# Residual and last MLP bias by accumulating DMA, and GpSimd in written order, in a one-core kernel of delta attention, MLP and gated feed-forward

## The chip, the cores and the metric

The kernel runs on one core of one Trainium2 chip. A core has five engines with a queue of instructions each: TensorE (PE, matmul; its weight loads are listed as PEld), VectorE (DVE), ScalarE (ACT), GpSimd (POOL) and SyncE (SP), which here only issues DMA transfers. An engine works its queue in order; between engines there are semaphores. The metric is the device time of one execution in microseconds; of a kernel, the median of its runs.

## What is computed

For each of 32 sequences of 512 tokens with 256 features, in float32:

```
x1 = layernorm(x)
x2 = x1 + delta(layernorm(x1)*dn_g + dn_b)            # q, k, v, rates lr; k normalized
     K = tril(k k^T, -1);  u = solve(I + K, v);  y = (q k^T)(lr * u);  y @ out_w + out_b
x3 = x2 + relu((layernorm(x2)*mn_g + mn_b) @ w1 + b1) @ w2 + b2
y  = x + x3                                           # the residual of the first half
out = y + (silu(h @ wg^T) * (h @ wu^T)) @ wd^T        # h = layernorm(y); wg, wu, wd: integers / 127
```

The change concerns the terms `x` and `b2` of `y`, which is held in the tile `a` of each sequence and becomes the output.

## The kernel before

Sequences go in pairs; there are 16. A tile is 128 partitions (tokens of a block) by 4 blocks by 256 features. Three pairs are in the machine at a time: the *older* pair ends its gated part (its down projection, `Down`), the *old* pair goes through MLP and gated part, the *new* pair through attention, and a *following* pair is loaded and normalized. `a` has six buffers, one for each sequence of three pairs.

The stages of one round, in the order in which the program writes them:

- `middle` (L1055): the down projections of the older pair (`plain` L976, `combined` L993) among the MLP of the old pair (`residual` L900, `mlp_in` L905, `mlp_out` L923, then `normed` and `turned` for stage "f"). Inverting the 32x32 blocks of the new pair (`invert` L632, on VectorE: L683, L689) is spread between as a side job (`Side`, paid by TensorE columns).
- `gated` (L931): gate and up products of the old pair, the longest stretch of matmuls (L940), then interleaved with `solution` (L1032), the block substitution of the new pair (`merge` L712, `solve` L770). In it a matmul `pr` is followed by `rhs` on VectorE (L788) and then by the matmul `pu` that reads it. As a side job the following pair is normalized (`normalized` L483).
- `values_phase` (L1174): the rest of the attention of the new pair, its layer norm for the MLP (`normed`, stage "m"), keys and Gram matrices of the following pair, whose diagonal blocks go through DRAM (`given`) to the inversion.

A layer norm that feeds a matmul ends in a transposition: VectorE turns 32x32 blocks (`Turn.chunk`, L460), SP writes them to DRAM (`way_m`, `way_f`, `way_a`) and fetches them as features by tokens (`hT_m`, `hT_f`, `ag`). Its reciprocal square root is on GpSimd (`r_m`, `r_f`, `rr`, L391), with a small product after it (`mr_m`, `mr_f`, L419).

In `normalized` the last feature of each token is replaced in `a` by a number that later products need; the feature itself is kept in `hlast` (L522, L523: two copies for each of four blocks) and put back in `gather` (L817).

`x` is loaded a second time for the residual (`fetch_residual`, L893, at the start of `values_phase`); GpSimd adds `b2`, spread over the partitions in `b2s`, and VectorE adds the tile to `a` in `residual`.

The down projection uses products of sums of blocks: `plain` multiplies the blocks of `hid` as they are, after which GpSimd replaces them by sums and differences (L987 to L990) for `combined`; GpSimd also adds parts of the result to `a` (L991, L1005, L1006).

What sets the order: TensorE, VectorE, ScalarE and SP execute in the order in which the program writes their instructions (`manual_schedule`, L1231). GpSimd is not in that list: a scheduler places its instructions, and had, for instance, moved L987 forward into the gated stage.

```
with tc.manual_schedule(engines={
    mybir.EngineType.PE, mybir.EngineType.DVE, mybir.EngineType.Activation, mybir.EngineType.SP
}):
```

Of the kernel before, what the change touches and what calls it, by code (L numbers as in the profile page):

```python
# [15 lines left out]
P = 128  # L16
# [6 lines left out]
def kernel(  # L23
# [297 lines left out]
    wdS = const.tile([P, NP, 7, P], F32, name="wdS")  # L321

    class Dequant:
        def __init__(self, src, name, tag, bufs, k):

            rows, self.cols = src.shape
            self.name, self.parts = name, []
            for r0 in range(0, rows // P, k):
                m = min(k, rows // P - r0)
                wi = wk.tile([P, m, self.cols], I32, tag=tag, name=f"{name}_i{r0}", bufs=bufs)  # L330
                self.parts.append((r0, m, wi))
            self.src = src

# [149 lines left out]
    def normalized(s):  # L483

        n = s.n
        mv = yield from stats(s.a, f"a{n}")


        vv = small.tile([P, 2, NT], F32, tag="vv", name=f"vv_{n}")
        nc.vector.tensor_scalar(vv[:, 0, :], mv[:, :, 1], EPS, None, ALU.add)  # L490
        nc.vector.scalar_tensor_tensor(
            out=vv[:, 1, :], in0=vv[:, 0, :], scalar=EPS, in1=mv[:, :, 1],
            op0=ALU.mult, op1=ALU.add,
        )
# [3 lines left out]
        nc.vector.tensor_scalar(nm, mv[:, :, 0], -1.0, None, ALU.mult)  # L498
# [12 lines left out]
        nc.vector.tensor_tensor(both, rr[:, 0, :], rr[:, 1, :], ALU.mult)  # L511
        s.r2 = small.tile([P, 2, NT], F32, tag="r2", name=f"r2_{n}", bufs=5)
        nc.vector.tensor_tensor(
            s.r2, vv, both.unsqueeze(1).to_broadcast([P, 2, NT]), ALU.mult
        )
        s.hlast = small.tile([P, NT, 1], F32, tag="hlast", name=f"hlast_{n}", bufs=5)
        for c in range(NT):
            nc.vector.tensor_scalar(
                s.a[:, c, :], s.a[:, c, :], left[:, c : c + 1], rr[:, 0, c : c + 1],
                ALU.subtract, ALU.mult,  # L520
            )
            nc.gpsimd.tensor_copy(s.hlast[:, c, :], s.a[:, c, C - 1 : C])  # L522
            nc.gpsimd.tensor_copy(s.a[:, c, C - 1 : C], s.r2[:, 1, c : c + 1])  # L523
            yield
        if n // NS == 1:
            s.ag = wk.tile([P, NF, T], F32, tag="aT", name=f"ag_{n}")
        else:
            s.ag = wk.tile([P, NF, T], F32, tag="feat", name=f"ag_{n}", bufs=4)
        if n >= 2 * NS:
            t = Turn(f"a{n}")  # L530
            for c in range(NT):
                t.chunk(s.a[:, c, :], c)
                yield
            t.send()
            for _ in range(4):
                yield
            t.fetch(s.ag)
        yield
# [74 lines left out]
    def norms(g, given, seqs):  # L613

        ss = small.tile([P, NS, NT], F32, tag="ss", name=f"ss_{g}", bufs=2)
        nc.sync.dma_start(
            ss.rearrange("p s t -> p (s t)"),
            given.rearrange("s b i e -> (s b) (i e)")[:, :: B + 1].rearrange("q t -> t q"),
        )
        yield  # L620
        yield 4
        kn = small.tile([P, NS, NT], F32, tag="kn", name=f"kn_{g}", bufs=2)
        nc.gpsimd.tensor_tensor(
            kn.rearrange("p s t -> p (s t)"), ss.rearrange("p s t -> p (s t)"), half, ALU.pow
        )
        yield 4
        for slot, s in enumerate(seqs):
            s.kn = kn[:, slot, :]
            nc.vector.tensor_tensor(s.kn, s.kn, s.r2[:, 0, :], ALU.mult)
        yield  # L630
# [259 lines left out]
        else:  # L890
            s.turn.fetch(s.hT)

    def fetch_residual(s):  # L893
        s.xt = wk.tile([P, NT, C], F32, tag="x", name=f"x_{s.n}")
        load_x(s.n, s.xt)
        nc.gpsimd.tensor_tensor(
            s.xt, s.xt, b2s.unsqueeze(1).to_broadcast([P, NT, C]), ALU.add
        )

    def residual(s):  # L900

        s.acc = s.a
        nc.vector.tensor_tensor(s.acc, s.acc, s.xt, ALU.add)

    def mlp_in(s, o):  # L905
        n = s.n
# [45 lines left out]
    class Down:  # L952
# [23 lines left out]
        def plain(self):  # L976
# [5 lines left out]
            x = wk.tile([P, 2, P], F32, tag="x2", name=f"x2_{name}")  # L982
            nc.scalar.copy(x, po[:, 1:3, :])
            first = self.acc[:, :, :P]

            A = self.A
            nc.gpsimd.tensor_tensor(A[1, 0], A[1, 0], A[1, 1], ALU.add)  # L987
            nc.gpsimd.tensor_tensor(A[0, 0], A[1, 0], A[0, 0], ALU.subtract)
            nc.gpsimd.tensor_tensor(A[0, 1], A[0, 1], A[0, 0], ALU.subtract)
            nc.gpsimd.tensor_tensor(A[1, 1], A[1, 1], A[0, 0], ALU.subtract)  # L990
            nc.gpsimd.tensor_tensor(first, first, x, ALU.add)  # L991

        def combined(self):  # L993
            name = f"{self.s.n}_{self.half}"
# [57 lines left out]
            next(gen)  # L1052
        return gens

    def middle(old, rest):  # L1055
# [21 lines left out]
        turned(one, "f")  # L1077
        todo(second[2:3])
        normed(two, "f")
        todo(second[3:])  # L1080
        return [d.store for d in rest]

    def last_middle(old, rest):
        one, two = old
        residual(one)
        rest[0].combined()
        mlp_in(one, 0)
        mlp_in(one, 1)
        residual(two)
        rest[1].combined()  # L1090
        mlp_out(one, 0)
        mlp_out(one, 1)
# [12 lines left out]
    def first_values(seqs, following, norms_, inverse, given):  # L1105
# [37 lines left out]
        for _ in turns:  # L1143
            pass
        for s in seqs:
            fetch_residual(s)
        whole = lambda gen: [None for _ in gen]
        whole(gather(one))
        whole(gather(two))
# [23 lines left out]

    def values_phase(seqs, following, prep, given, downs_left):  # L1174
        one, two = seqs
        for s in seqs:
            fetch_residual(s)
        whole = lambda gen: [None for _ in gen]
        if not following:
            units = iter(downs_left)  # L1180
            whole(gather(one))
            whole(gather(two))
            whole(through_values(one))
            next(units).plain()
# [5 lines left out]
            next(units).plain()  # L1190
            turned(one, "m")
            answer(two)
            normed(two, "m")
            next(units).plain()
            next(units).plain()
            turned(two, "m")
            return
        a, b = following
# [18 lines left out]
        keys(b, 0)  # L1217
        keys(b, 1)
        normed(one, "m")
        answer(two)  # L1220
        in_order(b)
        some(3)
# [6 lines left out]
        return sides_  # L1229

    with tc.manual_schedule(engines={  # L1231
        mybir.EngineType.PE, mybir.EngineType.DVE, mybir.EngineType.Activation, mybir.EngineType.SP
    }):

        first = pairs[0]
        gw = [wk.tile([P, GC], F32, tag="a", name=f"gw{f}", bufs=6) for f in range(NF)]
        quantized = [
            (Dequant(w_down, "wd", "hid", 2, 2), Combined().put),
            (Dequant(w_gate, "wg", "turn", 2, 4), whole_rows(wgT)),
            (Dequant(w_up, "wu", "x", 2, 4), whole_rows(wuT)),  # L1240
        ]
        load_a(first[0])
        gates = Gates(gw)
# [9 lines left out]
        b2s = const.tile([P, C], F32, name="b2s")  # L1253
        nc.scalar.dma_start(b2s, b2.partition_broadcast(P))
        for _ in normalized(first[0]):
            pass
        to_keys(first[0])
# [19 lines left out]
        for g in range(n_pairs):  # L1277
# [6 lines left out]
            else:  # L1284
                rest = downs(older) if older else []
                turned(old[1], "m")
                kn_side = Side(begun_[0], 10, 16 * 1024)
                inv_side = Side(
                    begun_[1], B * (4 + 3 * B // 2),
                    INVERT if older else INVERT_FIRST,  # L1290
                )
                stores = middle(old, rest)
                work = gated(old)
                for i in range(PLAIN):
                    next(work)
# [24 lines left out]
        for i, _ in enumerate(work):  # L1320
            if i == 5:
                turned(old[1], "f")
            if i in (3 * NH, 3 * NH + 2):
                rest.append(Down(old[0], len(rest)))
                rest[-1].plain()
        for h in range(NT // 2):
            rest.append(Down(old[1], h))
            rest[-1].plain()
        for d in rest:
            d.combined()  # L1330
            d.store()
# [29 lines left out]
```

## Time and profile before

| | us |
|---|---|
| median of 3 runs (2092.58, 2093.53, 4598.82) | 2093.53 |
| the profiled execution | 2090.19 |
| its span, first to last instruction | 2088.4 |
| mean granted TensorE clock | 0.995 of full |

Groups that the change touches (line, engine, count, busy us, mean ns):

| what | engine | count | busy us | mean ns |
|---|---|---|---|---|
| L896 x + b2 | POOL | 32 | 74.6 | 2348 |
| L903 a + x | DVE | 32 | about 48 (32 at the median of 1502) | 1502 |
| L522, L523 last feature | POOL | 128 + 128 | 34.3 + 26.5 | 268, 207 |
| L817 last feature back | POOL | 32 | 6.2 | 193 |
| L987 to L990 sums of blocks | POOL | 4 x 64 | 63.1, 79.5, 64.0, 64.0 | 1007 to 1243 |
| L991, L1005, L1006 result | POOL | 3 x 64 | 47.4, 33.0, 64.0 | 741, 516, 1000 |
| L623 kn | POOL | 16 | 31.3 | 1958 |

Transfers (KB each, median us from issue to landing): `x` 512, 5.5; `a` 512, 4.6; `hT_m` 512, 3.6; `hT_f` 512, 3.8; `ag` 512, 3.8; `blocks` 512, 5.1; `way_m` 128, 3.4; `given` 16, 1.5. GpSimd itself issues two transfers, both in the first 12 us: `row` (4 KB, 749 ns on the engine, 2.3 us to landing) and `unit` (128 KB, 659 ns, 5.4 us).

How to read it: a row of a group or a timeline gives start, duration, engine and line, operation, what is written from what, and in brackets how long the engine was idle before it and who released it. A wait row gives the total in us, the number of times and the longest. In a row of stretches the busy us of PE, PEld, DVE, ACT and POOL are followed by the granted clock, the share of the 16 DMA engines and GB/s. The ends of matmuls are modelled, and GpSimd's durations are rough.

### The profile page before, as it was taken

The numbers are of one execution on the slowest core, as the hardware profiler recorded it, in microseconds if no ns is written. First come the engines' busy times: TensorE is split into PE (matmuls) and PEld (weight loads), VectorE is DVE, ScalarE is ACT, GpSimd is POOL, SyncE is SP. The second block draws the span as 40 slices with busy tenths as digits, with TensorE's granted clock in tenths as the row PEclk, the third lists the DMA queues.
The fourth block names the chain that finished last, engine by engine and source line by source line (L and its number), as shares of the span: only waits on it lengthen the run. The fifth ranks groups of instructions, "written<-read, shape, count | busy, mean of one in ns | idle before, by whom it ended". The sixth has DMA issues, their size and how long they took to land.

```text
span 2088.4 us, 27547 instructions
## 1 busy us (share of the span) xinstructions
PE 2028.3 (97%) x9134; PEld 1373.5 (66%) x9134; DVE 1232.8 (59%) x3691; ACT 703.9 (34%) x1788; POOL 729.9 (35%) x1008
## 2 busy tenths in 40 slices
PE   5899999999999999999999999999999999999998
PEld 2565766757576675766767576675766767576675
DVE  3656474755747576474855747476474855747252
ACT  3333423324242343423334242343423334242231
POOL 3411332525224342432525224251422525124244
PEclk9999999999999999999999999999999999999999
DMA  3211332332324223332332324223332432323020
GB/s 90 83 34 28 84 98 62 109 90 56 91 71 127 63 74 89 92 90 62 107 95 54 94 69 128 62 74 89 87 95 62 113 88 54 94 69 107 22 61 21
DMA packets 249605, 163.90 MB, mean 78 GB/s; under 512 B 82129, under 2 KB 225112, under 8 KB 249464
## 3 DMA queue, kind: packets, MB, share of 16 engines
q1 hardware_dynamic: 246272, 160.30, 27.7%
q10 hardware_dynamic: 3112, 1.71, 0.3%
q8 instruction: 73, 1.20, 0.2%
q14 instruction: 68, 0.56, 0.1%
q0 software_dynamic: 80, 0.14, 0.0%
HBM read 96.02 MB, written 66.06 MB: 78 GB/s over the span
## 4 chain that ended last, share of the span: by engine, by line
PE 84%; DVE 7%; DMA 4%; issue 1%; POOL 1%; ACT 1%; SPq 1%; ACTq 0%; POOLq 0%; DVEq 0%
PE pup L940 16%; PE pgate L940 15%; PE pg L591 6%; PE po_d L844 5%; PE pf L805 5%; PE po_y L970 5%; PE pk L562 5%; PE po_x L970 4%; PE pr L784 4%; PE pa L911 4%; PE po_m L844 3%; PE pu L794 3%; PE pm L805 3%; PE pz L805 3%; DMA hT_f<-way_f 1%
## 5 line engine op out<-in xcount | busy, mean ns | idle before, releaser
L940 PE MATMUL pgate<-hT_f,wgT 128*128 128x512 f32 x768 | 366.5, 600 | 8.2 <-DMA hT_f<-way_f 6.3
L940 PE MATMUL pup<-hT_f,wuT 128*128 128x512 f32 x768 | 364.3, 596 | 0.0
L949 DVE TENSOR_TENSOR hid<-hid,pup 128x512 f32<-128x512 f32 x192 | 130.7, 681 | 243.7 <-PE pup L940 240.9
L947 ACT ACTIVATE hid<-pgate 128x512 f32<-128x512 f32 x192 | 113.7, 593 | 404.4 <-PE pgate L940 404.4
L940 PEld LDWEIGHTS pgate<-hT_f,wgT 128*128 128x128 f32 x768 | 142.4, 190 | 153.6 <-issue 135.6
L940 PEld LDWEIGHTS pup<-hT_f,wuT 128*128 128x128 f32 x768 | 143.1, 190 | 146.0 <-issue 139.7
L987 POOL TENSOR_TENSOR hid<-hid 128x384 f32<-128x384 f32 x64 | 63.1, 1007 | 383.0 <-DVE hid L949 383.0
L970 PEld LDWEIGHTS po_y<-wdS,hid 128*128 128x128 f32 x1536 | 176.5, 192 | 8.4 <-issue 6.0
L828 DVE TENSOR_TENSOR m<-pm,obrow 128x256 f32<-128x256 f32 x32 | 13.6, 424 | 280.5 <-ACT m L827 280.4
L970 PE MATMUL po_y<-wdS,hid 128*128 128x128 f32 x1536 | 176.8, 275 | 0.0
L391 POOL TENSOR_TENSOR r_m<-ve_m,neghalf 128x4 f32<-128x4 f32 x32 | 32.4, 1013 | 332.5 <-DVE nmn_m L417 332.4
L591 PE MATMUL pg<-kT 128*128 128x256 f32 (+3 forms) x512 | 144.1, 433 | 0.1
L970 PEld LDWEIGHTS po_x<-wdS,hid 128*128 128x128 f32 x1152 | 132.9, 192 | 8.3 <-issue 4.8
L970 PE MATMUL po_x<-wdS,hid 128*128 128x128 f32 x1152 | 134.1, 275 | 0.0
L591 PEld LDWEIGHTS pg<-kT 128*128 128x128 f32 x512 | 92.0, 190 | 52.9 <-issue 22.4
L562 PE MATMUL pk<-ag,wa 128*128 128x512 f32 x256 | 119.8, 602 | 0.9 <-ACT ag L443 0.9
L911 PE MATMUL pa<-hT_m,w1s 128*128 128x512 f32 x256 | 116.4, 597 | 0.8 <-DMA hT_m<-way_m 0.6
L844 PE MATMUL po_m<-w2s,act 128*128 128x256 f32 x512 | 116.3, 380 | 0.3
L805 PE MATMUL pf<-a,dp 128*128 128x256 f32 x512 | 113.1, 379 | 0.0
L422 ACT ACTIVATE h_f<-a,mr_f,r_f 128x256 f32<-128x256 f32 x112 | 60.6, 594 | 154.0 <-POOL mr_f L419 118.3
L805 PEld LDWEIGHTS pf<-a,dp 128*128 128x128 f32 x512 | 97.3, 190 | 19.6 <-issue 7.2
L689 DVE TENSOR_REDUCE beside<-xt 128x16 f32<-128x64 f32 (+14 forms) x225 | 103.8, 461 | 7.7
(202 smaller groups left out, 3458.0 us busy)
## 6 DMA issues: line engine op xcount, KB each, us to landing
a<-in_L_attn_x_dram SPq DMA_DIRECT2D x32, 512.0 KB, 4.6
x<-in_L_attn_x_dram SPq DMA_DIRECT2D x32, 512.0 KB, 5.5
out_dram<-a SPq DMA_DIRECT2D x64, 256.0 KB, 4.5
way_m<-turn_m SPq DMA_DIRECT2D x120, 128.0 KB, 2.6
hT_m<-way_m SPq DMA_DIRECT2D x30, 512.0 KB, 3.6
way_a<-turn_a SPq DMA_DIRECT2D x112, 128.0 KB, 2.3
ag<-way_a SPq DMA_DIRECT2D x28, 512.0 KB, 3.8
way_f<-turn_f SPq DMA_DIRECT2D x112, 128.0 KB, 2.3
```

Of the source, the lines that this page charges most:

```text
L562: nc.tensor.matmul(pk, lhsT=wa[:, f, ts(o, P)], rhs=s.ag[:, f, :], start=(f == 0), stop=(f == NF - 1),)
L591: nc.tensor.matmul(pg[:, :w], lhsT=s.kT[:, f, ts(j, P)], rhs=s.kT[:, f, j * P :], start=(f == 0), stop=(f == NF - 1),)
L689: nc.vector.tensor_reduce(xc[:, :, i : i + 2], t[:, :, :, :w], axis=AX.X, op=ALU.add)
L784: nc.tensor.matmul(pr, lhsT=s.go[j][:, ts(i - j - 1, P)], rhs=p_[:, j, :], start=(j == 0), stop=(j == i - 1),)
L805: nc.tensor.matmul(s.pp[:, o, :], lhsT=lhs[:, c, ts(o, P)], rhs=rhs[:, c, :], start=(c == 0), stop=(c == nk - 1),)
L844: nc.tensor.matmul(self.po[:, c % 2, :], lhsT=src[:, ts(c, P)], rhs=self.w[:, f, :], start=(f == 0), stop=(f == self.nk - 1),)
L911: nc.tensor.matmul(pa, lhsT=w1s[:, f, ts(o, P)], rhs=s.hT[:, f, :], start=(f == 0), stop=(f == NF - 1),)
L940: nc.tensor.matmul(pp, lhsT=w[:, f, ts(o, P)], rhs=s.hT[:, f, :], start=(f == 0), stop=(f == NF - 1),)
L947: nc.scalar.activation(natural(g), grouped(pp), AF.Silu)
L949: nc.vector.tensor_tensor(natural(g), natural(g), grouped(pp), ALU.mult)
L970: nc.tensor.matmul(po[:, i, :], lhsT=self.A[block][:, j, :], rhs=wdS[:, j, slot, :], start=(j == 0), stop=(j == NP - 1),)
L987: nc.gpsimd.tensor_tensor(A[1, 0], A[1, 0], A[1, 1], ALU.add)
```

## The change

- The residual no longer passes through SBUF. `biased` has SP copy `x` of a sequence into a DRAM tile `xb` and GpSimd issue a DMA that accumulates `b2`, read once for each of 512 rows, onto it. `residual` has GpSimd issue a DMA that accumulates `xb` onto `a`. The tile `x`, its two buffers and `b2s` go.
- `biased` is called in the fourth and fifth step of `solution`; `residual` of a pair's first sequence right after its `normed(one, "m")`, of the second in `middle` after two down projections.
- GpSimd joins the engines whose order is the written one. `plain` is divided: the sums of blocks are `mix`, and the additions to `a` are `own`, called in `combined`.
- `kn`'s side job has no rate any more: its square root is called before the last `combined` of `middle`, and VectorE's part when the job is finished before `solution`.
- `hlast` is filled by one copy for a sequence, after all four blocks are scaled, and the last feature is replaced by one copy.
- The integer weights are loaded into one tile in the place of a `hid` buffer and a new tile `whole`, in place of the tags `hid`, `turn` and `x`; `x2` has four buffers instead of two.

The order of TensorE and of ScalarE is unchanged but for the missing `b2s` load. VectorE's loses the two residual adds of a pair; of the four transposes of the following pair's first sequence two stand ahead of the first `rhs` pair and two behind it, where it had been all or three of them ahead.

```
-            nc.gpsimd.tensor_copy(s.hlast[:, c, :], s.a[:, c, C - 1 : C])
-            nc.gpsimd.tensor_copy(s.a[:, c, C - 1 : C], s.r2[:, 1, c : c + 1])
             yield
+        nc.gpsimd.tensor_copy(s.hlast, s.a[:, :, C - 1 : C])
+        nc.gpsimd.tensor_copy(s.a[:, :, C - 1 : C], s.r2[:, 1, :].unsqueeze(2))
+        yield
...
-    def fetch_residual(s):
-        s.xt = wk.tile([P, NT, C], F32, tag="x", name=f"x_{s.n}")
-        load_x(s.n, s.xt)
-        nc.gpsimd.tensor_tensor(
-            s.xt, s.xt, b2s.unsqueeze(1).to_broadcast([P, NT, C]), ALU.add
+    def biased(s):
+
+        s.xb = dram.tile([T, C], F32, tag="xb", name=f"xb_{s.n}", bufs=4)
+        nc.sync.dma_start(s.xb, x[s.n])
+        nc.gpsimd.dma_start(s.xb, b2.unsqueeze(0).to_broadcast([T, C]), accum_op=ALU.add)
+
+    def residual(s):
+
+        s.acc = s.a
+        nc.gpsimd.dma_start(
+            s.acc, s.xb.rearrange("(c p) d -> p c d", p=P), accum_op=ALU.add
         )
-
-    def residual(s):
-
-        s.acc = s.a
-        nc.vector.tensor_tensor(s.acc, s.acc, s.xt, ALU.add)
...
-            first = self.acc[:, :, :P]
+            self.x = wk.tile([P, 2, P], F32, tag="x2", name=f"x2_{name}", bufs=4)
+            nc.scalar.copy(self.x, po[:, 1:3, :])
+
+        def mix(self):
 
             A = self.A
             nc.gpsimd.tensor_tensor(A[1, 0], A[1, 0], A[1, 1], ALU.add)
             nc.gpsimd.tensor_tensor(A[0, 0], A[1, 0], A[0, 0], ALU.subtract)
             nc.gpsimd.tensor_tensor(A[0, 1], A[0, 1], A[0, 0], ALU.subtract)
             nc.gpsimd.tensor_tensor(A[1, 1], A[1, 1], A[0, 0], ALU.subtract)
-            nc.gpsimd.tensor_tensor(first, first, x, ALU.add)
+
+        def both(self):
+            self.plain()
+            self.mix()
+
+        def own(self):
+
+            acc = self.acc
+            first = acc[:, :, :P]
+            nc.gpsimd.tensor_tensor(first, first, self.x, ALU.add)
+            nc.gpsimd.tensor_tensor(acc[:, 0, :P], acc[:, 0, :P], self.e, ALU.add)
...
-            nc.gpsimd.tensor_tensor(acc[:, 0, :P], acc[:, 0, :P], self.e, ALU.add)
+            self.own()
...
-        todo(first[:2])
-        residual(one)
-        todo(first[2:3])
+        mix = [d.mix for d in rest]
+        todo(first[:1] + mix[:1])
+        todo(first[1:2] + mix[1:2])
+        residual(two)
+        todo(first[2:3] + mix[2:3])
         mlp_in(one, 0)
         mlp_in(one, 1)
         todo(first[3:])
-        residual(two)
         mlp_out(one, 0)
         mlp_out(one, 1)
+        todo(mix[3:])
...
         normed(two, "f")
+        next(kn_side.gen)
         todo(second[3:])
...
         normed(one, "m")
+        residual(one)
         answer(two)
...
     with tc.manual_schedule(engines={
-        mybir.EngineType.PE, mybir.EngineType.DVE, mybir.EngineType.Activation, mybir.EngineType.SP
+        mybir.EngineType.PE, mybir.EngineType.DVE, mybir.EngineType.Activation,
+        mybir.EngineType.SP, mybir.EngineType.Pool,
     }):
...
-                kn_side = Side(begun_[0], 10, 16 * 1024)
+                kn_side = Side(begun_[0], 0, 1)
...
                 for i, _ in enumerate(solution(new)):
                     next(work, None)
+                    if i in (3, 4):
+                        biased(new[i - 3])
```

More of the change, by code (lines that the diff above doesn't have):

```diff
@@ L323, with __init__ @@
     class Dequant:
-        def __init__(self, src, name, tag, bufs, k):
+        def __init__(self, src, name, place, k):
             rows, self.cols = src.shape
@@ L329, in __init__ @@
                 m = min(k, rows // P - r0)
-                wi = wk.tile([P, m, self.cols], I32, tag=tag, name=f"{name}_i{r0}", bufs=bufs)
+                wi = place[:, r0 * self.cols : (r0 + m) * self.cols]
+                wi = wi.rearrange("p (r c) -> p r c", r=m)
                 self.parts.append((r0, m, wi))
@@ L620, in norms @@
         yield
-        yield 4
         kn = small.tile([P, NS, NT], F32, tag="kn", name=f"kn_{g}", bufs=2)
@@ L891, in turned @@
             s.turn.fetch(s.hT)
-    def fetch_residual(s):
-        s.xt = wk.tile([P, NT, C], F32, tag="x", name=f"x_{s.n}")
-        load_x(s.n, s.xt)
-        nc.gpsimd.tensor_tensor(
-            s.xt, s.xt, b2s.unsqueeze(1).to_broadcast([P, NT, C]), ALU.add
-        )
+    def biased(s):
+        s.xb = dram.tile([T, C], F32, tag="xb", name=f"xb_{s.n}", bufs=4)
+        nc.sync.dma_start(s.xb, x[s.n])
+        nc.gpsimd.dma_start(s.xb, b2.unsqueeze(0).to_broadcast([T, C]), accum_op=ALU.add)
     def residual(s):
         s.acc = s.a
-        nc.vector.tensor_tensor(s.acc, s.acc, s.xt, ALU.add)
+        nc.gpsimd.dma_start(
+            s.acc, s.xb.rearrange("(c p) d -> p c d", p=P), accum_op=ALU.add
+        )
     def mlp_in(s, o):
@@ L981, in plain @@
             nc.scalar.copy(self.e, po[:, 0, :])
-            x = wk.tile([P, 2, P], F32, tag="x2", name=f"x2_{name}")
-            nc.scalar.copy(x, po[:, 1:3, :])
-            first = self.acc[:, :, :P]
+            self.x = wk.tile([P, 2, P], F32, tag="x2", name=f"x2_{name}", bufs=4)
+            nc.scalar.copy(self.x, po[:, 1:3, :])
+        def mix(self):
             A = self.A
@@ L1053, in begun, with middle @@
         return gens
-    def middle(old, rest):
+    def middle(old, rest, kn_side):
         one, two = old
@@ L1084, in last_middle @@
         one, two = old
-        residual(one)
+        for s in old:
+            residual(s)
         rest[0].combined()
@@ L1088, in last_middle @@
         mlp_in(one, 1)
-        residual(two)
         rest[1].combined()
@@ L1145, in first_values @@
         for s in seqs:
-            fetch_residual(s)
+            biased(s)
         whole = lambda gen: [None for _ in gen]
@@ L1175, in values_phase @@
         one, two = seqs
-        for s in seqs:
-            fetch_residual(s)
         whole = lambda gen: [None for _ in gen]
@@ L1183, in values_phase @@
             whole(through_values(one))
-            next(units).plain()
+            next(units).both()
             whole(through_keys(one))
@@ L1189, in values_phase @@
             normed(one, "m")
-            next(units).plain()
+            next(units).both()
             turned(one, "m")
@@ L1193, in values_phase @@
             normed(two, "m")
-            next(units).plain()
-            next(units).plain()
+            next(units).both()
+            next(units).both()
             turned(two, "m")
@@ L1219, in values_phase @@
         normed(one, "m")
+        residual(one)
         answer(two)
@@ L1236 @@
         gw = [wk.tile([P, GC], F32, tag="a", name=f"gw{f}", bufs=6) for f in range(NF)]
+        size = NH * C
+        places = [
+            wk.tile([P, 2, size], I32, tag="hid", name="integers"),
+            wk.tile([P, size], I32, tag="whole", name="integers_g", bufs=1),
+        ]
         quantized = [
-            (Dequant(w_down, "wd", "hid", 2, 2), Combined().put),
-            (Dequant(w_gate, "wg", "turn", 2, 4), whole_rows(wgT)),
-            (Dequant(w_up, "wu", "x", 2, 4), whole_rows(wuT)),
+            (Dequant(w_down, "wd", places[0][:, 0], 2), Combined().put),
+            (Dequant(w_gate, "wg", places[1], 4), whole_rows(wgT)),
+            (Dequant(w_up, "wu", places[0][:, 1], 4), whole_rows(wuT)),
         ]
@@ L1252 @@
         mnb = by_feature(mn_b, "mnb", nc.scalar)
-        b2s = const.tile([P, C], F32, name="b2s")
-        nc.scalar.dma_start(b2s, b2.partition_broadcast(P))
         for _ in normalized(first[0]):
@@ L1291 @@
                 )
-                stores = middle(old, rest)
+                stores = middle(old, rest, kn_side)
                 work = gated(old)
@@ L1324 @@
                 rest.append(Down(old[0], len(rest)))
-                rest[-1].plain()
+                rest[-1].both()
         for h in range(NT // 2):
             rest.append(Down(old[1], h))
-            rest[-1].plain()
+            rest[-1].both()
         for d in rest:
```

## The prediction

> **What bounds the kernel now.** First the page: the busy shares and the chain of waits.
>
> ```profile
> PE 2028.3 (97%) x9134; PEld 1373.5 (66%) x9134; DVE 1232.8 (59%) x3691; ACT 703.9 (34%) x1788; POOL 729.9 (35%) x1008
> PE 84%; DVE 7%; DMA 4%; issue 1%; POOL 1%; ACT 1%; SPq 1%; ACTq 0%; POOLq 0%; DVEq 0%
> ```
>
> TensorE is busy 2028.3 of 2088.4 us, so all other engines together leave it idle for 60.1 us. Then TensorE's own waits, longest first:
>
> ```profile
> PE tp_a L441 <- DVE a L518: 21.8, 1, 21.8
> PE pw L730 <- DVE xparts L723: 11.5, 16, 6.3
> PE pgate L940 <- DMA hT_f<-way_f: 6.3, 6, 1.7
> ...
> PE pgate L940 <- DVE a L1000: 1.7, 2, 0.9
> ...
> PE pa L911 <- DMA hT_m<-way_m: 0.6, 3, 0.2
> ```
>
> The 21.8 is the first load of the kernel. In the steady pairs (about 125 us each, 16 pairs) under 1 us per pair is idle. So little can be won: the change removes no matmul. What matters is which operand arrives just in time, because any lateness of it is TensorE's. I took the timelines of one pair, from 740 to 850 us, engine by engine:
>
> ```profile
> 751.86 0.38 SPq L473 DMA_DIRECT2D hT_m<-way_m  x1
> 760.80 0.38 SPq L473 DMA_DIRECT2D hT_m<-way_m  x1
> 755.59 3.70 PE L911 MATMUL pa<-hT_m,w1s 128*128 128x512 f32 x8
> 764.59 3.60 PE L911 MATMUL pa<-hT_m,w1s 128*128 128x512 f32 x8
> ```
>
> An hT_m fetch lands 3.6 us (median of 30) after its issue: at 755.5 and 764.4 here. TensorE starts on them at 755.59 and 764.59. Over six pairs read in this way the first has 0.0 to 0.2 us to spare, the second 0.1 to 1.2, mean 0.7.
>
> ```profile
> 816.01 1.65 POOL L391 TENSOR_TENSOR rr<-vv,neghalf 128x8 f32<-128x8 f32 x1 [3.01 <-DVE nm L498]
> 818.49 1.38 DVE L518 TENSOR_SCALAR a<-a,left,rr 128x256 f32<-128x256 f32 x4
> 819.79 1.21 DVE L460 STREAM_TRANSPOSE turn_a<-a 128x256 f32<-128x256 f32 x3
> 820.92 0.65 DVE L949 TENSOR_TENSOR hid<-hid,pup 128x512 f32<-128x512 f32 x1
> 821.49 0.86 DVE L788 SCALAR_TENSOR_TENSOR rhs<-a,kn,pr 128x256 f32<-128x256 f32 x2
> 822.64 1.03 PE L794 MATMUL pu<-rhs,yfull 128*128 128x256 f32 x4
> ```
>
> This is the other narrow place. VectorE transposes the next sequence (L460), which needs GpSimd's copies into `a`; behind it in VectorE's queue stands the `rhs` that `pu` reads at 822.64. The first `rhs` ends at 821.9.
>
> **The change, part by part.**
>
> *Off GpSimd and VectorE.* 32 bias adds L896 at 2.35 us (74.6 us), 32 residual adds L903 at 1.5 us (48 us) and 192 of 256 last-feature copies go. None was waited for by TensorE, with one exception: the second L903 of a pair (764.50, 1.12 us) stands in the chain that ends in hT_f, directly ahead of the first `a<-a,po_m`. Taking it out brings hT_f 1.1 us earlier. That can win no more than TensorE waits there: 6.3 + 1.7 = **-8 us**. The 32 loads of `x` (839.4 in this pair) go too; beside them only `ag` moves, fetched at 839.0 and read at 863.15, so **0**.
>
> *kn.* The square roots move to a fixed place on GpSimd, and VectorE's two small products (0.22 us) move from 775.46, where there was slack, to just ahead of the transposes L722 and L723 that release `pw`. TensorE waits there in every pair already: 15 x 0.22 = **+3 us**.
>
> *GpSimd's order.* L987, which ran early (L987 at 804), now starts after the second `mr_m`. From 749.8 the four-step mixes take 4 x 0.97 us each: done at 753.8, 757.7, then 4 us after the second residual's issue, all ahead of `r_f`, which VectorE releases at 769.8 (now 768.7). The fourth mix follows `r_f` and ends near 774; its `po_y` is last, at about 779.5. The one-buffer `uv` is released 0.2 us later at worst. **0**; with 2 us more of GpSimd work before 768 it would delay `r_f` and so hT_f.
>
> *The copy of x in DRAM.* SP issues it after the `yfull` transfers (801.98 for 3.82 us, so from 805.8); at the 5.5 us of an `x` load it lands near 812. GpSimd comes to wait for it after `rr`, at 817.65. Behind that wait stand both bias issues and then the two copies into `a`: 5 us of cover, **0**.
>
> *The two bias issues, per pair with a following pair (14 of them).* They stand on GpSimd between `rr` and the copies. With d us each, VectorE's first `rhs` ends at 817.65 + 2d + 0.4 (two copies at 0.19) + 0.8 (two transposes) + 0.65 (L949) + 0.43, and TensorE is late by 2d - 2.7 us. It decides from d = 1.36. The trace has two GpSimd DMA issues, at the start of the run: 4 KB in 4 rows took 749 ns, 128 KB in 128 rows took 659 ns. These move 512 rows and read the destination too. Bounds: as those rows, 0.7 (no loss: the copies then wait for L518 at 819.87 and 0.5 us is still spare; a gain is excluded, nothing waits for it now); by rows, 4 x 0.659 = 2.64. I take 2.64: TensorE 2.6 us late, 14 x 2.6 = **+36 us**.
>
> A rule bears on the same row. The Trainium skill, "SBUF — State Buffer", section "SBUF: two separate sides", says that descriptors of a GpSimd DMA are written over the port pair that VectorE's two-port operations lock, and gives 620 ns alone against 3100 ns beside a VectorE copy. The 659 and 749 ns were taken with VectorE nearly idle; at 817.65 it is in its four L518 and is busy 80% of 815 to 820. No row shows such an issue beside VectorE. By the rows the term is 0; by the rule d = 3.1, 3.5 us late, +49. My 2.64 lies between, nearer to the rule.
>
> *The residual transfers.* The first is issued once ACT has read `a` (744.5), the second after two mixes, at 757.7 + d, near 760. VectorE needs them at the first `a<-a,po_m` of each sequence, 765.5 and 774.9: over 14 us later, so nobody waits for them. But they share the DMA engines with the fetches above. By stretches:
>
> ```profile
> 745.00:750.00 5.00, 5.00 (x23) 3.38 (x22) 4.37 (x19) 3.06 (x10) 1.21 (x2) 1.00 0.45 108
> 750.00:755.00 5.00, 5.00 (x47) 5.00 (x46) 3.46 (x5) 3.31 (x9) 4.54 (x4) 1.00 0.48 118
> 755.00:760.00 5.00, 5.00 (x22) 2.97 (x22) 1.03 (x3) 2.15 (x6) 4.92 (x7) 1.00 0.81 210
> 760.00:765.00 5.00, 5.00 (x29) 4.37 (x28) 4.59 (x15) 0.70 (x3) 4.92 (x7) 1.00 0.37 107
> ```
>
> The last two columns are the DMA share and GB/s. The first residual falls where the engines are half free; the second falls on the second hT_m fetch (760.80 to 764.4) after a stretch that is 81% full. The nearest row of the same size is the `x` load, 5.5 us; no row shows an accumulating transfer. Lower bound for the fetch: no delay, since 19% to 63% is free; upper: its moving part, 3.6 less the 1.5 us of the smallest transfer (`given`, 16 KB), lasts twice as long, +2.1. As the residual also reads its destination I take 2.1, less the 0.7 to spare: 1.4 x 14 = **+20 us**. The first fetch may lose up to 0.5, inside the same lateness.
>
> *Ends.* In the last pair the residuals stand behind all four mixes: some 2 us of wait near 2006, **+2**. Copying the last feature once per sequence delays the first transposes by 0.4 us, within the 0.5 spare above. The integers in other tiles, four `x2` buffers and the missing `b2s` load touch nothing that anyone waits for in this trace: 0; the cover is the DMA wait before L342, 2.3 us once.
>
> Sum: -8 + 3 + 36 + 20 + 2 = +53 us. The profiled execution took 2090.2 us (its span 2088.4 and 1.8 around it); the median of the runs shown, 2093.5, is 3.3 above it. The forecast for the median is 2093.5 + 53 = **2147 us**, 2.5% slower.
>
> **The rivals.**
>
> *Cheap issues (2109).* If d stays under 1.36 the bias issues cost nothing; the transfers still collide: -8 + 3 + 20 + 1 = +16. For it: 128 rows cost no more than 4. Against it: four times the rows, a second read, VectorE busy.
>
> *Nothing collides (2089, the other side).* The second residual's transfer, between 758 and 765, fits into the free 19% to 63% of the DMA engines, and hT_m is not delayed. The place is the fetch at 760.80, the price 0 instead of 20, and it decides when the fetch loses less than its 0.7 us. With cheap issues: -8 + 3 = -5. Against it: the skill's "DMA: Bandwidth & Descriptors", section "Issuing engines are not separate DMA queues", has transfers of all issuers interleave on the same 16 engines, and `way_m` in this trace lands in 1.9 to 5.8 us, the long ones where `blocks` moves beside it.
>
> *Slow accumulation (2190).* If the residual's moving part takes three times that of a load, the first one reaches over 751.86 and delays `given`, `blocks` and the first hT_m, which has nothing to spare: 2 us there and 1.5 more at the second, 49 instead of 20; with d = 3.1, 49 instead of 36, and 4 at the end: -8 + 3 + 49 + 49 + 4 = +97.
>
> *A wait at the issue itself.* If the copy of `x` in DRAM took over 12 us to land, GpSimd would stand before it with the copies into `a` queued behind; this adds to any case and is in the upper range.
>
> **How the numbers follow.** What a measurement of this kernel can tell from no change is about 2%, 42 us: faster is under 2051.6, slower over 2135.4. Forecast 0.43, slow accumulation 0.17, cheap issues 0.28, nothing collides 0.12. Slower: 0.37 of the forecast's 0.43 (d above 2.2), all of 0.17 and 0.02 of cheap issues = 0.56. Faster by over 2% would need 42 of TensorE's 60 idle us, of which 22 are the first load; I leave it 0.03, out of the case without collisions, for stalls inside the busy figure, whose ends are modelled. Within: 0.41. The range runs from the case without collisions to slow accumulation, 2088 to 2195, which leaves out half of the first and half of the last, under 0.2; the forecast's own range, d from 2 to 3.1, is 2128 to 2160.
>
> **What would show it.** In the changed profile: the GpSimd DMA issues above 1.36 us each and, among TensorE's waits, `pu <- rhs` in 14 pairs with over 1 us each; with d under 1.36 that row is missing. `pa <- DMA hT_m` grows from 0.6 to some 20 us and its landing from 3.6 to 5 or more; if it stays, nothing collided. `pgate <- DMA hT_f` goes to near nothing, `pw <- xparts` gains some 3 us. The forecast is wrong if issues are cheap, or if a wait that I cost at nothing (`po_m <- a`, `pk <- ag`) appears.

## The result, and the profile after

| | before | after |
|---|---|---|
| median of the runs, us | 2093.39 | 2111.83 |
| profiled execution, us (its span) | 2090.2 (2088.4) | 2112.7 (2110.9) |
| mean granted TensorE clock | 0.995 | 0.993 |

The ratio after to before is 1.0094, 95% interval 1.0067 to 1.0121: about 0.9% slower, where 2.5% slower was forecast. (One of the four runs before took 4598.82 us; the ratio leaves it out.) First the changed kernel's page, busy shares and GpSimd's DMA queue (packets, MB, share of 16 engines' span):

```profile
PE 2032.5 (96%) x9134; PEld 1373.0 (65%) x9134; DVE 1186.5 (56%) x3659; ACT 703.4 (33%) x1788; POOL 668.3 (32%) x848
q0 software_dynamic: 33872, 33.69, 15.5%
```

VectorE and GpSimd lost 46 and 62 us of work, and the kernel became slower: neither was the bound. GpSimd's queue q0, nearly empty before (80 packets), now holds the DMA engines for 15.5% of the span. TensorE's waits in the changed kernel (total, times, longest):

```profile
PE pa L913 <- DMA hT_m<-way_m: 19.5, 23, 1.9
PE pw L731 <- DVE xparts L724: 12.9, 16, 6.4
PE tp_f L442 <- ACT turn_f L423: 6.3, 1, 6.3
PE pg L593 <- ACT kT L571: 1.9, 1, 1.9
...
PE pgate L942 <- DVE a L1013: 1.8, 3, 0.7
...
PE pgate L942 <- DMA hT_f<-way_f: 0.6, 1, 0.6
```

Against before: `pa` +18.9, `pw` +1.4, `tp_f` +3.0 (3.3 before), `pg` +1.9 (no row before; it stands at 32.42 us, in the start-up), the two `pgate` rows -5.6, and the first load -0.4 (21.4). Together +19.2 us. TensorE's busy time is 4.2 us more, in part at a lower clock behind the `tp_f` wait (see "Ends" below). That is 23.4 of a span 22.5 longer. A row `pu <- rhs` does not exist. GpSimd's own transfers, by line (busy us, mean ns of one, then idle time before them):

```profile
L903 POOL DMA_DIRECT2D a<-xb x32 | 43.1, 1364 | 47.9 <-ACT h_m L423 42.1 <-ACT turn_m L423 5.7
L898 POOL DMA_DIRECT2D xb<-in_L_attn_b_dram x32 | 35.0, 1282 | 0.1
```

A bias issue took 1.28 us, not 2.64; the two of a pair stand back to back and overlap a little, so that 32 hold GpSimd for 35.0 us, 1.09 each. The changed kernel's transfers by issue (KB each, median us to landing):

```profile
xb<-in_L_attn_b_dram POOLq DMA_DIRECT2D x32, 512.0 KB, 17.8
a<-xb POOLq DMA_DIRECT2D x32, 512.0 KB, 7.2
...
way_m<-turn_m SPq DMA_DIRECT2D x120, 128.0 KB, 4.0
hT_m<-way_m SPq DMA_DIRECT2D x30, 512.0 KB, 3.9
way_a<-turn_a SPq DMA_DIRECT2D x112, 128.0 KB, 6.8
```

Before (the 3.4 given for `way_m` ahead of the prediction is the median of `way_m` and `hT_m` taken together):

```profile
way_m<-turn_m SPq DMA_DIRECT2D x120, 128.0 KB, 2.6
...
way_a<-turn_a SPq DMA_DIRECT2D x112, 128.0 KB, 2.3
```

`hT_m` landed in 3.6 us before. One pair of the changed kernel, from its timelines (start, duration, engine; in brackets TensorE's wait):

```profile
753.36 1.38 POOL L903 DMA_DIRECT2D a<-xb  x1 [2.96 <-ACT h_m L423]
753.57 1.88 SPq L468 DMA_DIRECT2D way_m<-turn_m  x4
758.57 1.74 SPq L611 DMA_DIRECT2D given<-gd  x4
761.33 0.57 SPq L474 DMA_DIRECT2D hT_m<-way_m  x1
766.50 1.31 POOL L903 DMA_DIRECT2D a<-xb  x1
769.60 0.38 SPq L474 DMA_DIRECT2D hT_m<-way_m  x1
765.11 3.70 PE L913 MATMUL pa<-hT_m,w1s 128*128 128x512 f32 x8 [0.84 <-DMA hT_m<-way_m]
774.64 3.67 PE L913 MATMUL pa<-hT_m,w1s 128*128 128x512 f32 x8 [0.37 <-DMA hT_m<-way_m]
```

Each `hT_m` fetch has a residual transfer just ahead of it. The first one starts together with `way_m`, which the fetch must wait for: from `given` to the fetch it is 2.8 us here, 1.9 before (749.96 to 751.86):

```profile
749.96 1.73 SPq L609 DMA_DIRECT2D given<-gd  x4
```

The second overlaps the fetch itself. Over all pairs the waits ahead of the first `pa` sum to 11.7 us and those ahead of the second to 7.9.

### The profile page after: what moved, and what is told of

The parts are those of the page before. It is cut to its first block, busy times and chain, and to the rows that moved or that the text cites. A ratio compares the mean times of both kernels' runs of the same rounds, so it can differ in the third digit from the quotient of the medians.

```text
span 2110.9 us, 27504 instructions
## 1 busy us (share of the span) xinstructions
PE 2032.5 (96%) x9134; PEld 1373.0 (65%) x9134; DVE 1186.5 (56%) x3659; ACT 703.4 (33%) x1788; POOL 668.3 (32%) x848
## 3 DMA queue, kind: packets, MB, share of 16 engines
q0 software_dynamic: 33872, 33.69, 15.5%
## 4 chain that ended last, share of the span: by engine, by line
PE 82%; DMA 8%; DVE 5%; POOL 2%; ACT 1%; issue 1%; SPq 1%; ACTq 0%; POOLq 0%; DVEq 0%
PE pup L942 16%; PE pgate L942 15%; PE po_y L972 6%; PE pg L593 6%; PE pf L806 5%; PE pk L564 5%; PE po_d L845 5%; PE pa L913 4%; PE pr L785 4%; DMA hT_m<-way_m 4%; PE po_m L845 3%; PE pu L795 3%; PE pm L806 3%; PE pz L806 3%; PE po_x L972 2%; DMA way_m<-turn_m 2%
## 5 line engine op out<-in xcount | busy, mean ns | idle before, releaser
L913 PE MATMUL pa<-hT_m,w1s 128*128 128x512 f32 x256 | 117.8, 602 | 19.9 <-DMA hT_m<-way_m 19.5
L760 POOL MEMSET xparts<- 32x128 f32 x32 | 6.3, 197 | 382.3 <-PE pw L751 382.3
## 6 DMA issues: line engine op xcount, KB each, us to landing
xb<-in_L_attn_b_dram POOLq DMA_DIRECT2D x32, 512.0 KB, 17.8
```

Source lines behind the costliest of these rows:

```text
L913: nc.tensor.matmul(pa, lhsT=w1s[:, f, ts(o, P)], rhs=s.hT[:, f, :], start=(f == 0), stop=(f == NF - 1),)
```

## The experiments

Ratios are to the kernel before, run on the same chip; the changed kernel's is 1.0094. One percent is 20.9 us. The changed kernel's own interval is wide, 1.0067 to 1.0121: by the times alone, e1, e2, e5 and e6 are not told apart from it, and what is said of them rests on the waits.

| run | what differs from the changed kernel | ratio (95%) |
|---|---|---|
| e1_no_one | no residual of the first sequence | 1.0073 (1.0061 to 1.0085) |
| e2_no_two | none of the second | 1.0063 (1.0046 to 1.0080) |
| e3_no_both | neither | 0.9992 (0.9983 to 1.0001) |
| e4_bias_parts | bias in 4 transfers a sequence | 1.0531 (1.0511 to 1.0551) |
| e5_no_bias | no bias accumulation | 1.0102 (1.0086 to 1.0118) |
| e6_two_later | second residual a mix later | 1.0072 (1.0056 to 1.0088) |
| e7_shifted | both residuals later | 1.0330 (1.0312 to 1.0349) |
| e8_vector_early | before, second add moved up | 0.9995 (0.9985 to 1.0006) |
| e9_plain | same bytes, no accumulation | 1.0019 (1.0011 to 1.0027) |
| e10_bias_halves | bias in 2 transfers | 1.0194 (1.0171 to 1.0217) |
| e11_loaded | plain load, VectorE adds | 0.9988 (0.9981 to 0.9995) |

**Is it the residual transfers?** Three runs leave them out, all but those of the last pair.

```
         normed(one, "m")
-        residual(one)          # e1, e3
+        one.acc = one.a
...
-        residual(two)          # e2, e3
+        two.acc = two.a
```

> Leaves out the residual (x and the last bias) of the first sequence of every pair but the last; the bias accumulation in DRAM stays. Collision theory: the first residual's transfer delays way_m, given and through them the first hT_m fetch; TensorE's waits for hT_m before the first pa of a pair (0.4 to 1.9 us, together some 13 of the 19.5 us) go, those before the second stay: about 2112 - 13 = 2099 us. Rival, that the second transfer alone collides as the prediction had it: 2112 within 3. Rival, that the lateness is from GpSimd's new order and not from transfers: 2112.

> Leaves out the residual of the second sequence of every pair but the last. Collision theory: the waits before the second pa (0 to 1.4 us, some 7 of the 19.5 us) go and the second hT_m fetch lands in 3.6 us again instead of 4.9: about 2112 - 7 = 2105 us. The prediction's own split (nearly all of the 20 us is the second's): 2112 - 19 = 2093 us. Order of GpSimd as the cause: 2112.

> Leaves out both residuals but in the last pair; bias accumulation in DRAM and GpSimd's order stay. Collision theory: all waits for hT_m go, 2112 - 19 = 2093 us, about the time before; if the two terms are not independent, less than the sum of the two runs that leave out one. Order of GpSimd, or the bias issues, as the cause: 2112, with the waits for hT_m still there.

Without both, the time is that of the kernel before, and in the list of TensorE's waits the row `pa <- hT_m` is gone:

```profile
PE tp_a L442 <- DVE a L519: 22.8, 1, 22.8
PE pw L731 <- DVE xparts L724: 12.9, 16, 6.4
PE tp_f L442 <- ACT turn_f L423: 2.8, 1, 2.8
PE pg L593 <- ACT kT L571: 1.9, 1, 1.9
```

So the residual transfers carry all of the loss: 1.0094 to 0.9992, 21 us. GpSimd's written order, still in this run, costs nothing on balance. The two runs that leave out one of them, e1 and then e2:

```profile
PE pa L913 <- DMA hT_m<-way_m: 11.7, 14, 1.2
PE pa L913 <- DMA hT_m<-way_m: 11.5, 14, 1.3
```

Without the first residual the ratio is 4 us lower, not 13, a miss in size; without the second it is 6 us lower, near the 7 foreseen. The two are not independent. Without the first, all of the 11.7 us are ahead of the second `pa`, where the changed kernel has 7.9; without the second, all of the 11.5 are ahead of the first, as many as in the changed kernel. When the first `pa` is late, TensorE reaches the second `pa` later too, and part of the second fetch's lateness is hidden behind that; take the first residual away and it shows in full. (In e1 a `tp_f` wait of 5.7 us stays as well, which is the second residual's, see below.)

**Do the bias issues cost nothing, and was the path to `rhs` read rightly?** One run leaves the bias out, two cut each issue into smaller ones.

```
-        nc.gpsimd.dma_start(s.xb, b2.unsqueeze(0).to_broadcast([T, C]), accum_op=ALU.add)
+        for r in range(0, T, P):              # e4; e10: steps and sizes of 2 * P; e5: nothing
+            nc.gpsimd.dma_start(
+                s.xb[r : r + P], b2.unsqueeze(0).to_broadcast([P, C]), accum_op=ALU.add
+            )
```

> Leaves out the last bias: the accumulation of b2 onto the copy of x in DRAM is not issued; copy and residual transfers stay. Theory: at 1.28 us an issue is under the 1.36 us from which TensorE would be late, so the issues cost nothing, and the transfer (17.8 us to land, way_a beside it 6.8 us instead of 2.3) has slack too: the time of the changed kernel, 2111 within 3. Rival, that the slowed way_a or the crowded DMA engines cost TensorE something that the waits do not name: 2100 to 2106.

> The bias accumulation of each sequence in two transfers of 256 rows. From 1.28 us for 512 rows and 0.85 for 128 an issue of 256 rows takes about 1.0, so d = 2.0 for a sequence, and the model gives 2d - 2.7 = 1.3 us at pu <- rhs in 14 pairs: +18, 2129 us, if a stall of 1.3 us leaves TensorE's clock alone. If TensorE loses clock after any stall, as it did after the 4 us ones (2.6 us more each), +35 or more: 2146 us. If the path has more slack than 2.7 us: 2111.

> The bias accumulation of each sequence in four transfers of 128 rows instead of one of 512. If an issue costs 0.66 us as the first rows of the trace have it, a sequence's issues take d = 2.6 us on GpSimd, and by the prediction's model TensorE is late by 2d - 2.7 = 2.6 us in 14 pairs at pu <- rhs: 2112 + 36 = 2148 us. If the price is by the rows and not by the instruction (1.28 us for 512 rows), d stays near 1.3 to 1.6 and the time within 2112 to 2120. If the model of the path is wrong (more slack at rhs than 2.7 us), the issues take 2.6 us and the time stays at 2112.

Without the bias the time does not move (1.0102 against 1.0094, intervals overlapping). With halves, GpSimd's timeline and TensorE's wait:

```profile
840.27 3.71 POOL L899 DMA_DIRECT2D xb<-in_L_attn_b_dram  x4
```

```profile
PE pu L795 <- DVE rhs L789: 12.5, 14, 0.9
```

Four issues hold GpSimd for 3.71 us; by the prediction's model TensorE is 3.71 - 2.7 = 1.0 late; 0.9 was measured, in the 14 pairs named. The time rose by 1.0 percentage point, 21 us, against 18 foreseen. That agrees better than its parts: the wait is 12.5 us of it, and TensorE's busy time is 5.6 us longer (2038.1). With quarters, first the same wait and then the timeline:

```profile
PE pu L795 <- DVE rhs L789: 55.7, 14, 4.0
```

```profile
866.05 6.80 POOL L899 DMA_DIRECT2D xb<-in_L_attn_b_dram  x8
875.22 2.04 PE L795 MATMUL pu<-rhs,yfull 128*128 128x256 f32 x4 [3.98 <-DVE rhs L789]
```

6.80 - 2.7 = 4.1 by the model, 4.0 measured. (The 2148 us expected of this run were too low: an issue took 0.85 us and not 0.66, and a lower clock was not foreseen.) So the model of the path holds at both points. The price of an issue hardly falls with its rows: in one pair 2 of 512 rows took 2.16 us in sum, 4 of 256 took 3.71, 8 of 128 took 6.80. That is 1.08, 0.93 and 0.85 us each. The quarters' total of 91 us over the changed kernel is more than 14 x 4.0 = 56: the matmuls after the stall are slow. `pu` took 1.03 us for four just before, 2.04 here. In stretches of the same run the column behind GpSimd's busy time is the granted clock:

```profile
870.00:875.00 5.00, 1.24 (x3) 0.19 (x1) 1.66 (x5) 0.60 (x1) 3.25 (x6) 0.89 1.00 67
875.00:880.00 5.00, 4.78 (x8) 2.86 (x9) 2.62 (x10) 1.50 (x4) 0.00 (x0) 0.50 1.05 64
```

TensorE runs at half speed for about 5 us on average after the stall, which costs some 2.6 us more per pair, 36 in all: 56 + 36 = 92. Its busy time in that run is 2069.0 us, 36.5 above the changed kernel's.

**Can the transfers be placed better?**

```
         todo(first[:1] + mix[:1])
+        residual(one)                         # e7; not after normed(one, "m")
         todo(first[1:2] + mix[1:2])
-        residual(two)                         # e6, e7
         todo(first[2:3] + mix[2:3])
+        residual(two)                         # e6, e7
```

> The second residual is issued after the third mix instead of before it, some 4 us later (near 771 in the pair that starts TensorE's first pa at 765), about when the second hT_m fetch is half done. Collision theory: that fetch lands in 3.6 to 4 us again, the waits before the second pa go, those before the first stay: as without the second residual, 2102 to 2104 us. Rival, that the transfer only collides with something later (hT_f's turn or the a that po_m is added to, where 7 us of transfer from 772 leave 4 us): 2111 or more, with a wait po_m or pgate in place of pa.

> Both residuals moved: the first behind the first mix (issue near 762, just after the first hT_m fetch is issued; its a is needed near 773), the second behind the third mix (near 772). Collision theory: neither fetch shares its time with a residual, waits for hT_m fall from 19.5 to under 6 us: 2090 to 2098 us. Rival, that the transfers collide wherever they stand in this crowded stretch: 2105 to 2111, first residual too late for po_m included.

With the second one alone moved, the `pa` waits fall from 19.5 to 12.3, and what is left is mostly ahead of the first `pa`; the ratio is 5 us lower, less than foreseen and inside the changed kernel's interval. The first residual's place was misjudged: 2162 us, where 2090 to 2098 were expected. In the shifted kernel's timelines:

```profile
784.84 1.37 POOL L903 DMA_DIRECT2D a<-xb  x1
783.95 0.58 SPq L637 DMA_DIRECT2D blocks<-given  x1
785.21 3.55 SPq L468 DMA_DIRECT2D way_m<-turn_m  x4
794.42 0.38 SPq L474 DMA_DIRECT2D hT_m<-way_m  x1
798.15 5.37 PE L913 MATMUL pa<-hT_m,w1s 128*128 128x512 f32 x8 [2.33 <-DMA hT_m<-way_m]
```

The first `hT_m` is now on time, but the residual moves beside `blocks` and the second `way_m`. That one lands in up to 8.4 us (6.5 at most in the changed kernel), SP waits for it, and the second fetch is issued 9.2 us after `way_m` began, where it was 5.3 in the changed kernel's pair above. The `pa` waits rise to 43.9 us, and behind nearly every long one TensorE is slow again. What had to be kept free here is the whole chain of transfers, `way_m` and `blocks` included, not only the last one.

**Bytes or accumulation?** The transfer stays, with the same size and the same places in GpSimd's order, but writes plainly into a spare tile.

```
-            s.acc, s.xb.rearrange("(c p) d -> p c d", p=P), accum_op=ALU.add
+            spare[:, 0], s.xb.rearrange("(c p) d -> p c d", p=P)
```

> Leaves the residual out: at the same two places GpSimd issues a transfer of the same 512 KB from the same DRAM copy, but a plain one into a tile that nobody reads. If the bytes on the DMA engines are what hT_m loses to, most of the 21 us stays: 2105 to 2111 us. If the accumulation is (each row read twice, at a slower rate), they go: 2089 to 2095 us, with a landing near the 5.5 us of a plain load instead of 7.2.

Its page, the issue row and the queue:

```profile
q0 software_dynamic: 21584, 33.69, 12.9%
...
x<-xb POOLq DMA_DIRECT2D x32, 512.0 KB, 4.4
```

Only about 6 of the 21 us stay (1.0019 against 0.9992), and most of these are not the bytes': in the last pair the second transfer waits for the first to leave the one spare tile, which TensorE feels.

```profile
PE pa L912 <- DVE a L1012: 2.9, 1, 2.9
```

The four `pa` matmuls behind that stall take 3.65 us instead of 1.88. So the bytes alone cost a few us at most. For the second residual this shows that accumulating is what costs: it is issued 12.9 us after the first `way_m` in both kernels, and TensorE waits 1.3 us for `hT_m` in all, where it waited 11.7 with the accumulating one alone (e1). For the first it is only in part shown: the spare tile does not wait for ScalarE to have read `a`, so the transfer starts earlier:

```profile
743.31 0.87 POOL L904 DMA_DIRECT2D x<-xb  x1 [0.31 <-issue]
745.83 2.30 SPq L468 DMA_DIRECT2D way_m<-turn_m  x4
```

It is 2.5 us ahead of `way_m`, where the accumulating one was 0.2 ahead, and at its 4.4 us it is over while `way_m` is still being issued. What the earlier start alone is worth was not measured. The same megabytes take 12288 packets fewer, 384 a transfer, and land in 4.4 us instead of 7.2. From the queue's share: 15.5% of 2110.9 us less the bias (10.1% of 2090.1 in the last run below, where the bias has the queue alone) is 327 - 211 = 116 us, or 3.6 us of all 16 engines for each of 32 residuals. The run without the bias, where the residuals have the queue alone, gives the same 116 us (5.5% of 2112.7). A plain one, 12.9% of 2090.6 less the same 211 for the bias, takes 1.8.

**Two versions without the accumulating residual.** One moves a single line of the kernel before, the other loads the biased copy of `x` as before `x` was loaded.

```
         residual(one)                         # e8, in the kernel before
+        residual(two)
...
+            nc.sync.dma_start(s.xt, s.xb.rearrange("(c p) d -> p c d", p=P))   # e11
...
-            s.acc, s.xb.rearrange("(c p) d -> p c d", p=P), accum_op=ALU.add
+        nc.vector.tensor_tensor(s.acc, s.acc, s.xt, ALU.add)   # both, before the third mix
```

> The kernel before with one line moved: VectorE adds the second residual directly after the first, in the stretch in which it waits 4.4 us for blocks, instead of ahead of the first a<-a,po_m. No transfer, no new order on GpSimd. If the second add was what made hT_f late, as the prediction's first step has it, 6.3 + 1.7 us of waits go: before - 7, about 2084 us. Rival, that hT_f is late for another reason: before within 2.

> The changed kernel with the residual moved by a plain load of the biased copy of x into a spare tile (on SP, at the start of the values stage, where the kernel before loaded x), and added by VectorE, both sequences one after the other in the stretch in which VectorE waits for blocks. GpSimd's order, the one copy of the last feature and the bias in DRAM stay. If the accumulating transfers are all that the change costs: the time before within 3 us, 2088 to 2094. Rival, that GpSimd's order or the bias transfer has a price of its own: 2096 or more. Below 2086 it would beat both kernels.

The line moved in the kernel before gave no measurable gain. The `hT_f` waits fell, but from 6.3 + 1.7 to 3.3 + 1.6 us, and those for `hT_m` grew by 0.6; the rest has another cause, which was not followed. The second version is at 0.9988: everything of the change stays but the accumulating residual, and it is 2.5 us below before, ahead of both kernels by a hair.

## Why the prediction was wrong, point by point

- **The failed step: "The two bias issues", +36.** The threshold was right (late by 2d - 2.7, confirmed at 3.71 and 6.80 us of issues), the size of d was wrong. Between the row's 0.7 and "by rows, 4 x 0.659 = 2.64" I took the upper one. The measured d is 1.28, about 1.1 in effect where two overlap: 2.2 us for a pair, 0.5 under the threshold, so the term is 0. The price follows the instruction: 0.85 us at 128 rows and 1.08 at 512. With 0 in its place the sum is -8 + 3 + 20 + 2 = +17, and +18.4 was measured: the rival "cheap issues", at 2109. That the two agree so closely is in part luck, since the terms that stay are off in both directions (below).
- **The rule that leaned on that step.** The Trainium skill, "SBUF — State Buffer", section "SBUF: two separate sides", has such a DMA's descriptors wait for VectorE's two-port operations, and gives 3100 ns instead of 620 for the DMA beside a VectorE copy. The prediction took that figure as the time of the issue on GpSimd. Here the bias issues run while VectorE scales `a` (four L519 from 828.21 in a pair whose issues run from 827.33 to 829.49), and none of 32 took more than 1.52 us; the four L519 took 1.72 us there, 1.38 before. So the figure does not carry over to these short instructions, and it should not have pulled d upward. Nor was VectorE "in its four L518" at 817.65, as the prediction reads the timeline: they start at 818.49.
- **"The residual transfers", +20.** Right in sum (`pa` +18.9), wrong in its split and its reason, so the sum is luck. The first transfer, put at up to 0.5 inside the second's lateness, alone makes TensorE wait as long as the second alone does (11.5 and 11.7 us), and it does so through `way_m` and `given` rather than through the fetch: the path that the rival "slow accumulation" names, at 0.8 us a pair instead of 2. The landing of `hT_m`, foreseen at 5 or more, is 3.9 at the median. A plain transfer of the same bytes costs a few us at most (e9); the accumulating one holds the DMA engines twice as long. I had only a load's row to go by.
- **"Off GpSimd and VectorE", -8.** 5.6 came off in the profile of the changed kernel. The same edit without transfers (e8) takes 3.1 us off that wait and no measurable time off the kernel, so this term was too large.
- **"kn", +3:** `pw` grew by 1.4, half of it.
- **"Ends", +2:** near in size by luck, wrong in place. In the last pair 0.3 us is lost. The loss is in the first pair, where nothing was foreseen: the second residual delays `given` and so `blocks`, and VectorE, which stands before `blocks` in its written order, comes late to everything behind. VectorE's and TensorE's rows there, before and after:

```profile
141.06 0.36 DVE L649 RECIPROCAL few<-blocks 128x32 f32<-128x32 f32 x1 [5.64 <-DMA blocks<-given]
151.82 0.33 PE L441 MATMUL tp_f<-ident,turn_f 128*128 128x128 f32 x1 [2.77 <-ACT turn_f L422]
...
145.85 0.36 DVE L650 RECIPROCAL few<-blocks 128x32 f32<-128x32 f32 x1 [11.40 <-DMA blocks<-given]
156.66 2.81 PE L442 MATMUL tp_f<-ident,turn_f 128*128 128x128 f32 x8 [6.30 <-ACT turn_f L423]
```

Without the second residual the waits are 8.08 and 2.94. The granted clock behind the 6.30 us stall is 0.50 from 155 to 160 and 0.74 from 160 to 165, where before it was 0.72 and 1.00.

- **What I costed at nothing** stayed at nothing: GpSimd's order and the copies of the last feature (e3, e11), the copy of `x` in DRAM, and `ag`, though its `way_a` lands in 6.8 us instead of 2.3 (`pk <- ag` still 0.9 us). The new `pg <- kT` wait of 1.9 us in the start-up is still there in e3, is gone in e9 and e10, and was not explained.

## What to carry to other kernels

Work taken off engines that are not the bound won nothing here (e3), and the transfers that replaced it were not free: look at which chain of transfers ends just in time, with all its links, before adding one beside it. Where a cost decides only above a threshold and the nearest rows lie on both sides of it, one cheap measurement of that cost is worth more than any choice between the ends. An accumulating DMA from DRAM onto SBUF held the DMA engines here for twice as long as a plain one of the same size (3.6 us against 1.8); that is one size in one kernel, and a better starting point than a load's row.

## What was not expected of the hardware

- **Accumulating between DRAM tensors is slow and delays what runs beside it.** The bias accumulation of 512 KB, its source read again for each row, landed in 17.8 us and held all 16 engines for 6.6 (211 us for 32). In stretches of the changed kernel right behind the two issues, the DMA share is full at some 60 GB/s (last two columns):

```profile
825.00:830.00 5.00, 5.00 (x22) 2.89 (x21) 3.98 (x14) 3.82 (x13) 3.77 (x4) 1.00 0.12 12
830.00:835.00 5.00, 5.00 (x16) 2.75 (x15) 4.28 (x13) 1.89 (x5) 0.38 (x2) 1.00 1.10 68
835.00:840.00 5.00, 5.00 (x19) 3.42 (x18) 2.58 (x8) 1.47 (x6) 1.55 (x1) 1.00 1.03 61
```

  `way_a` beside it needs 6.8 us; without the bias it needs 2.2. It costs TensorE nothing here: `pk` waits no longer for `ag`, and the run without the bias is no faster.
- **A stall costs TensorE more than its length.** After stalls of 4.0 us the clock was 0.50, for about 5 us on average (the 2.6 us lost in each pair); after one of 2.33 us in the shifted kernel it was 0.71, then 0.50, and eight `pa` matmuls took 5.37 us instead of 3.6:

```profile
798.00:800.00 2.00, 1.85 (x3) 0.82 (x4) 1.90 (x10) 0.00 (x0) 0.73 (x1) 0.71 1.19 189
800.00:802.00 2.00, 2.00 (x4) 0.78 (x3) 1.37 (x4) 0.72 (x2) 1.84 (x4) 0.50 0.23 38
```

  After the 0.9 us stalls of the halves the mean clock stayed at 0.993. The Trainium skill, "TensorE: Matmul & The Clock Gate", section "Part 1: The HAM clock gate (the "warmup" mystery)", names half speed after an idle window of about 3.4 us; the 4.0 us stalls agree, and the 2.33 us one shows that less can be enough. So does one of 2.06 us in the halves' run (eight `pa` in 5.40 us), while behind one of 2.81 us in the shifted kernel they took 3.67. So the length of a stall alone does not decide, and no threshold is shown here.
